# Newton of a layer norm on ScalarE with its products out of PSUM, and eleven of sixteen key tiles kept in an attention kernel

## The chip, the cores and the metric

The kernel runs on one core of a Trainium2 chip. The metric is the device time of one execution in microseconds. It was timed three times; a further execution was taken with the hardware profiler, and the profile is of that one.

## The reference, cut to what matters

The input is x, 2 batches of 2048 positions with 512 features, and one condition vector per batch. A first block (a state space layer and a feed-forward layer, both modulated by the condition) gives a new x. The change touches only the second block, an attention layer with 16 heads of 32 features:

```python
h = _sln(hidden, ...)                      # layer norm, then gamma * ln + beta from the condition
qkv = (h @ Wqkv.T + bqkv).reshape(B, N, num_heads, hd, 3)
energy = einsum('bhqd,bhkd->bhqk', q, k)
att = softmax(energy, axis=-1) / D ** 0.5  # exact: the maximum of each row is taken off first
out = einsum('bhqk,bhkd->bhqd', att, v)    # then back to (B, N, D)
h1 = out @ Wp.T + bp + hidden
h2 = _sln(h1, ...)                         # the last norm
return h2 + h1
```

All of it is in float32. The scores of one head are 2048 x 2048, so they never exist as a whole.

## The kernel before, in words

**Two parts.** The first part runs the state space layer, the feed-forward layer and the projections to queries, keys and values, chunk by chunk, and writes keys, queries and values to DRAM. It ends near 1470 us and isn't changed, but for the helper `rsqrt`, which it shares. The second part, from L698 on, is the attention and what follows it.

**Blocks.** The attention runs over 64 blocks: 2 batches, 8 pairs of heads, 4 chunks of 512 queries. In a block there are 16 tiles of 128 keys. Scores are computed with keys on the partitions: a tile of scores `s` is 128 keys x (2 heads x 512 queries), two matmuls (`raw_scores`, L754). A score plus its shift (minus the maximum of its query) goes through the exponential, and is then multiplied with the values (`weighted`, L834), which sums over keys in one PSUM bank `o`. A row of ones among the values gives the sums of the softmax.

**Two ways for a key tile.** The maximum over all keys must be known before an exponential is taken.

- The first NX = 10 tiles are *kept*: `keep` computes the scores once, ScalarE copies them to a buffer of the pool `ring` (L765), and VectorE takes a running maximum over key tiles, elementwise, from the scores in PSUM (L770, none for the first tile). Later `take_off` adds the shift in place on GpSimd (L813), and ScalarE takes the exponential (L824).
- The other NY = 6 tiles are scored *twice*: `across` computes them with queries on the partitions (two matmuls of NY x 64 = 384 columns, L779) for VectorE to reduce along the row (L784), eight times a block; `make` computes them again with keys on the partitions, and VectorE adds the shift while it leaves PSUM (L819).

`turn_run` transposes the running maximum on TensorE, one head at a time (L790), and VectorE reduces it to one column per 128 queries (L791, L794). `spread` transposes the result (pt_neg, L801), copies it out on ScalarE (neg_row, L803), and sends it through DRAM to all partitions with two DMAs on SP's queue (L805, L807); the tile that lands is the `shift`.

**Periods.** The order is written out by hand: each block has NP = 8 periods, and the loop at the end of the function goes over periods j. In period j it does, in this order: what is due at j (`after`); for the block at hand `make`; for the block AHEAD = 15 periods later one `across`; the first exponential; the `keep` of one or two tiles; the second exponential; what is due at j + 0.5 (`closing`); the take-offs for the next period; and `weighted` for the two tiles of the period before. `twice` names the two of the eight periods of keeping in which two tiles are kept; these coincide with periods that use two kept tiles and make none. So every period has two score tiles, one `across` and two tiles of weighting. Counted from the block at hand, two tiles are kept in periods 0 and 4. Each engine runs its instructions in the order in which they were written.

**PSUM.** Scores `s` have two buffers of two banks, `m` (across) one of two banks, `o` one bank, and one bank with tag `pt` serves in turn for the transposes of `turn_run` and `spread`, for projections and for the norm.

**Closing.** When all heads of a chunk are done, each tile of 128 queries is closed: `fetch` loads it, `divide` takes the softmax sums out on GpSimd, `project` multiplies with Wp (eight instructions, L905), `residual` adds x (L911), `statistics` takes mean and variance (L917, L920), `deviation` finds 1/sqrt for two query tiles at once by three Newton steps on VectorE (L932, `rsqrt` at L119 to L127, L938), `last_norm` applies scale and shift on ScalarE, and `close` multiplies by the gain row `g_row`, adds `t_row` and the residual on GpSimd and stores. Batch 0 is closed during the attention of batch 1, two query tiles in three blocks, with `add_t` on GpSimd as well. For the last batch (`LB`) the norm goes to PSUM and the gain is multiplied on VectorE (L949, L950). The last chunk is closed by `end_last`, all four tiles at once, out of PSUM.

Of the kernel before, what the change touches and what calls it, by code (L numbers as in the profile page):

```python
# [8 lines left out]
F32 = mybir.dt.float32  # L9
# [3 lines left out]
I32 = mybir.dt.int32  # L13
AF = mybir.ActivationFunctionType
ALU = mybir.AluOpType
# [24 lines left out]
def tile_s5_block_then_sln_attention(  # L40
# [48 lines left out]
    four = const.tile([P, NB], F32, name="four")  # L89

# [25 lines left out]
    def rsqrt(v, y, n, turns=(0, 3)):  # L116

        if turns[0] == 0:
            nc.vector.tensor_scalar(  # L119
                y.bitcast(I32), v.bitcast(I32), -0.5, float(0x5F3759DF), ALU.mult, ALU.add  # L120
            )
        for _ in range(*turns):
            a = small.tile([P, n], F32, name="rs_a", tag=f"rs_a{n}")
            nc.vector.tensor_mul(a, y, y)  # L124
            b = small.tile([P, n], F32, name="rs_b", tag=f"rs_b{n}")
            nc.vector.scalar_tensor_tensor(b, a, -0.5, v, ALU.mult, ALU.mult)  # L126
            nc.vector.scalar_tensor_tensor(y, b, 1.5, y, ALU.add, ALU.mult)  # L127
# [572 lines left out]
    NX = 10  # L700
# [4 lines left out]
    ring = ctx.enter_context(tc.tile_pool(name="ring", bufs=21, side="right"))  # L705
# [202 lines left out]
    def residual(b, qt):  # L908

        o4, h, py = held[b, qt]  # L910
        nc.vector.tensor_add(h, py, h)  # L911
        held[b, qt] = h, o4.rearrange("p g q -> p (g q)")

    def statistics(b, qt):
        h, ht = held[b, qt]
        st = small.tile([P, 6], F32, name="st3")
        nc.vector.bn_stats(st, h)  # L917
        if qt % 2 == 0:
            held[b, "mv"] = small.tile([P, 2, 2], F32, name="mv3")
        nc.vector.bn_aggr(held[b, "mv"][:, qt % 2, :], st)  # L920

    def add_t(b, qt):
        h, ht, *_ = held[b, qt]
        nc.gpsimd.tensor_tensor(ht, h, ending[b][1], ALU.add)

    def deviation(b, qt, parts=(0, 1)):

        mv = held[b, "mv"]
        if 0 in parts:
            v = small.tile([P, 2], F32, name="v3")  # L930
            y = small.tile([P, 2], F32, name="scale3", bufs=3)
            nc.vector.tensor_scalar(v, mv[:, :, 1], EPS, None, ALU.add)  # L932
            held[b, "vy"] = v, y
        v, y = held[b, "vy"]
        rsqrt(v, y, 2, {(0,): (0, 1), (1,): (1, 3), (0, 1): (0, 3)}[tuple(parts)])
        if 1 in parts:
            shift = small.tile([P, 2], F32, name="shift3", bufs=3)
            nc.vector.scalar_tensor_tensor(shift, mv[:, :, 0], -1.0, y, ALU.mult, ALU.mult)  # L938
            for i in range(2):
                h, ht = held[b, qt - 1 + i]  # L940
                held[b, qt - 1 + i] = h, ht, y[:, i : i + 1], shift[:, i : i + 1]

    def last_norm(b, qt):

        h, ht, scale, shift = held[b, qt]
        y = work.tile([P, D], F32, name="y")
        if b == LB:
            z = ps.tile([P, CH], F32, name="z", tag="pt")
            nc.scalar.activation(z, h, AF.Identity, bias=shift, scale=scale)  # L949
            nc.vector.tensor_tensor(y, z, ending[b][0], ALU.mult)  # L950
        else:
            nc.scalar.activation(y, h, AF.Identity, bias=shift, scale=scale)
        held[b, qt] = h, ht, y

    def close(b, qt):

        h, ht, y = held.pop((b, qt))
        if b == LB:
            ht = h
            nc.gpsimd.tensor_tensor(h, h, ending[b][1], ALU.add)  # L960
        else:
            nc.gpsimd.tensor_tensor(y, y, ending[b][0], ALU.mult)
        nc.gpsimd.tensor_tensor(y, y, ht, ALU.add)
        nc.sync.dma_start(out[b, qt * P : (qt + 1) * P, :], y)
# [65 lines left out]
    def end_last(o):  # L1030
# [17 lines left out]
        for i in range(2):  # L1048
            for t in (2 * i, 2 * i + 1):
                nc.tensor.matmul(  # L1050
                    ends["py", i][:, t % 2, :], on[:, t * P : (t + 1) * P], ends["w"], start=False, stop=True
                )
            for t in (2 * i, 2 * i + 1):
                st = small.tile([P, 6], F32, name="st3")
                nc.vector.bn_stats(st, ends["py", i][:, t % 2, :])  # L1055
                nc.vector.bn_aggr(mv[:, t, :], st)
            nc.scalar.copy(hts[i], ends["py", i])
            for t in range(2):
                nc.gpsimd.tensor_tensor(hts[i][:, t, :], hts[i][:, t, :], t_row, ALU.add)
# [6 lines left out]
        for t in range(TT):  # L1066
            qt = LC * TT + t
            y, ht = ends["h"][t // 2][:, t % 2, :], hts[t // 2][:, t % 2, :]
            nc.scalar.activation(
                y, ends["py", t // 2][:, t % 2, :], AF.Identity,  # L1070
                bias=shift[:, t : t + 1], scale=scale[:, t : t + 1],
            )
            nc.vector.tensor_tensor(y, y, g_row, ALU.mult)  # L1073
            (nc.gpsimd if t % 2 else nc.vector).tensor_tensor(y, y, ht, ALU.add)  # L1074
            nc.sync.dma_start(out[LB, qt * P : (qt + 1) * P, :], y)
# [5 lines left out]
    AHEAD = 15  # L1081
    NP = 8
    twice = (3, 7)
# [18 lines left out]
    def after(j, what, *args):  # L1102

        due.setdefault(j, []).append((what, args))
# [6 lines left out]
    FIRST = -AHEAD - 8  # L1111
    OPEN = -4
    for i, n in enumerate(opens):
        free = NP * (max(m for m in range(N) if pair_of[m] == i - 2) + 1) if i > 1 else FIRST
        after(max(free if i > 1 else FIRST, NP * n - AHEAD - 11), load_k, i)
        after(max(OPEN + 2, NP * n - 9), load_v, i)
    for n in range(N):
        after(max(FIRST + 1 + n, NP * n - AHEAD - 6), load_q, n)
        after(NP * n - AHEAD + NP + 1, turn_run, n, 0)
        after(NP * n - AHEAD + NP + 3, turn_run, n, 1)  # L1120
        after(NP * n - AHEAD + NP + 4, spread, n)
    for b in range(NB):
        for c in range(NQ):
# [22 lines left out]
            for t in range(TT):  # L1146
                qt = c * TT + t
                if b == LB:
                    k = j + 3 + 2 * t
# [148 lines left out]
```

## Time and profile before

| what | us |
|---|---|
| median of three executions (range) | 3531.95 (3527.56 to 3532.42) |
| the profiled execution | 3530.68 |
| its span, first to last instruction | 3528.9 |
| TensorE busy in the span | 3382.5 |
| VectorE, ScalarE, GpSimd busy | 2219.1, 1899.6, 2006.8 |
| first pt_neg to last pt_neg (blocks 0 to 63) | 1469.7 to 3426.0 |
| one ordinary block, pt_neg to pt_neg | 28.8 |

The page of a profile counts an engine as busy while an instruction of it runs. In a view of stretches the columns are the stretch, its length, busy time and number of instructions of TensorE matmuls, weight loads, VectorE, ScalarE and GpSimd, the granted TensorE clock as a share, the busy share of the DMA engines and GB/s. In a timeline the columns are the start, the duration, engine, source line, operation, output<-input and count; the brackets give idle time ahead of it and what ended it. In a view of waits a row says who waited for whom, for how long in total, how often, and the longest. PEld is the weight load of TensorE, which runs beside the matmul before it. The ends of matmuls are modelled, so spacing between starts tells more than their durations. L lines are those of the kernel before.

### The profile page before, as it was taken

What the parts mean: (1) busy time and instruction counts of PE and PEld (TensorE: products, weight loads), DVE (VectorE), ACT (ScalarE), POOL (GpSimd) and SP (SyncE); (2) the same over time, 40 slices, a digit from 0 to 9 for tenths busy, and PEclk for the clock granted to TensorE, in tenths of its full rate; (3) what the DMA queues carried; (4) which work ended last, traced back from release to release, by engine and by line L of the source; (5) the groups of instructions that cost most, each with busy time, mean ns of one, the idle gap of its engine ahead of it and who ended that gap; (6) DMA issues with size and microseconds to landing.
All of it is one profiled execution on the core that took longest, in us unless ns stands there. A gap on an engine that the chain in (4) does not pass through costs nothing. (4 is left out here: it accounts for less than half of the span.)

```text
span 3528.9 us, 34023 instructions
## 1 busy us (share of the span) xinstructions
PE 3382.5 (96%) x11772; PEld 1536.7 (44%) x11772; DVE 2219.1 (63%) x2946; ACT 1899.6 (54%) x2150; POOL 2006.8 (57%) x1028
## 2 busy tenths in 40 slices
PE   7999999999999999899999999999999999999986
PEld 4444444444444444444444444444444444444432
DVE  6233232323232212589999999998888888888865
ACT  2111112111111111488888888888788888888743
POOL 4223131313131311288877888888798888888765
PEclk8999999999999999999999999999999999999988
DMA  8001111111111012332313222232233323323232
GB/s 298 1 30 42 48 39 45 39 49 38 48 36 42 33 43 75 100 71 65 71 48 76 70 66 63 55 72 67 71 83 85 90 71 79 84 71 79 72 92 78
DMA packets 201539, 236.91 MB, mean 67 GB/s; under 512 B 89754, under 2 KB 118938, under 8 KB 197272
## 3 DMA queue, kind: packets, MB, share of 16 engines
q1 hardware_dynamic: 201368, 234.74, 24.4%
q8 instruction: 93, 1.52, 0.2%
q14 instruction: 78, 0.64, 0.1%
HBM read 166.77 MB, written 67.76 MB: 66 GB/s over the span
## 5 line engine op out<-in xcount | busy, mean ns | idle before, releaser
L813 POOL TENSOR_TENSOR x<-x,shift 128x1024 f32<-128x1024 f32 x640 | 1506.6, 2396 | 237.3 <-DMA shift<-flat 177.1
L765 ACT COPY x<-s 128x1024 f32<-128x1024 f32 x640 | 635.3, 1013 | 291.5 <-PE s L754 288.9
L754 PE MATMUL s<-qs,ks 128*128 128x512 f32 x2048 | 699.6, 432 | 48.1 <-DVE run L770 44.3
L824 ACT ACTIVATE x<-x 128x1024 f32<-128x1024 f32 x640 | 676.8, 1058 | 16.5 <-POOL x L813 16.5
L834 PE MATMUL o<-x,v 128*64 128x512 f32 x2560 | 673.4, 622 | 0.6 <-ACT x L824 0.6
L770 DVE TENSOR_TENSOR run<-s,run 128x1024 f32<-128x1024 f32 x512 | 625.2, 1221 | 56.6 <-ACT x L765 39.0
L819 DVE TENSOR_TENSOR pT<-s,shift 128x1024 f32<-128x1024 f32 x384 | 467.5, 1217 | 57.9 <-PE s L754 52.6
L784 DVE TENSOR_REDUCE top<-m 128x1 f32<-128x768 f32 x512 | 486.0, 949 | 25.7 <-PE m L779 25.3
L754 PEld LDWEIGHTS s<-qs,ks 128*128 128x128 f32 x2048 | 346.4, 189 | 303.9 <-DVE run L770 133.2
L488 PE MATMUL ph<-fT,w_sb 128*128 128x512 f32 x1024 | 462.4, 596 | 0.0
L501 PE MATMUL po<-w_sb,hid 128*128 128x512 f32 x1024 | 460.3, 592 | 0.0
L824 ACT ACTIVATE pT<-pT 128x1024 f32<-128x1024 f32 x384 | 407.6, 1061 | 59.2 <-DVE pT L819 51.8
L834 PE MATMUL o<-pT,v 128*64 128x512 f32 x1536 | 399.4, 598 | 13.4 <-ACT pT L824 13.4
L492 ACT ACTIVATE hid<-ph,vec 128x512 f32<-128x512 f32 x128 | 88.1, 688 | 594.8 <-PE ph L488 594.8
L159 DVE SCALAR_TENSOR_TENSOR lo<-pk,vec,hi 128x512 fp32r<-128x512 f32 x64 | 48.1, 751 | 502.7 <-ACT hi L158 497.5
L488 PEld LDWEIGHTS ph<-fT,w_sb 128*128 128x128 f32 x1024 | 192.9, 191 | 228.2 <-issue 228.2
L779 PE MATMUL m<-ks,qs 128*128 128x384 f32 x1024 | 286.1, 361 | 5.2 <-DVE top L784 3.5
L501 PEld LDWEIGHTS po<-w_sb,hid 128*128 128x128 f32 x1024 | 190.7, 190 | 221.5 <-issue 221.5
L435 POOL TENSOR_TENSOR m<-m,m 128x512 f32<-128x512 f32 x8 | 13.1, 1644 | 448.5 <-DVE m L433 448.5
L834 PEld LDWEIGHTS o<-x,v 128*64 128x64 f32 x2560 | 140.1, 137 | 265.2 <-issue 163.0
L158 ACT ACTIVATE hi<-pk,vec 128x512 fp32r<-128x512 f32 x64 | 44.0, 688 | 392.5 <-PE pk L531 392.5
L511 POOL TENSOR_TENSOR x<-x,gated 128x512 f32<-128x512 f32 x32 | 39.6, 1271 | 354.3 <-DVE gated L510 354.3
(249 smaller groups left out, 2844.9 us busy)
## 6 DMA issues: line engine op xcount, KB each, us to landing
ks<-kd SPq DMA_DIRECT2D x128, 256.0 KB
qs<-qd SPq DMA_DIRECT2D x512, 64.0 KB
shift<-flat SPq DMA_DIRECT2D x64, 512.0 KB
x<-in_x SPq DMA_DIRECT2D x8, 1024.0 KB
w_sb<-in_w SPq DMA_DIRECT2D x8, 1024.0 KB
x<-x SPq DMA_DIRECT2D x8, 1024.0 KB
kd<-hi SPq DMA_DIRECT2D x32, 256.0 KB
kd<-lo SPq DMA_DIRECT2D x32, 256.0 KB
```

The lines of the kernel that those rows point to most:

```text
L488: nc.tensor.matmul(ph, w1_sb[:, k, f * P : (f + 1) * P], fts[b, c][:, k, :], start=k == 0, stop=k == KC - 1)
L492: nc.scalar.activation(hids[f], ph, AF.Gelu_apprx_tanh, bias=vec[:, V_B1 + f : V_B1 + f + 1], scale=1.0)
L501: nc.tensor.matmul(pos[b, c][:, t, :], hid[:, t * P : (t + 1) * P], w2_sb[:, f, :], start=f == 0, stop=f == FC - 1,)
L754: nc.tensor.matmul(s[:, e, :], kst[pair_of[n], e][:, kt * P : (kt + 1) * P], qst[n][:, e, :], start=True, stop=True,)
L765: nc.scalar.copy(x, s)
L770: nc.vector.tensor_tensor(runs[n], s, kept[n, 0] if kt == 1 else runs[n], ALU.max)
L779: nc.tensor.matmul(m[:, i, :YW], qst[n][:, e, t * P : (t + 1) * P], kst[pair_of[n], e][:, k : k + YW], start=True, stop=True,)
L784: nc.vector.tensor_reduce(tops[n][:, j, 0:1], m[:, :, :YW], AX.XY, ALU.max, negate=True)
L813: nc.gpsimd.tensor_tensor(x, x, shifts[n], ALU.add)
L819: nc.vector.tensor_tensor(x, s, shifts[n], ALU.add)
L824: nc.scalar.activation(x, x, AF.Exp)
L834: nc.tensor.matmul(outs[n][64 * e : 64 * e + 64, :], v[:, kt, e : e + 2, :], x[:, e, :], start=first, stop=final,)
```

## The change

Six things change together.

- NX is 11: eleven tiles are kept, five are scored twice, `across` has two matmuls of 320 columns, and the ring has 22 buffers. AHEAD is 14, so the maxima are found 14 periods ahead. `twice` has three entries; counted from the block at hand, two tiles are kept in periods 2 (the first two tiles of a block), 5 and 7. The loads keep their old periods, now written as numbers; `spread` stays three periods ahead of its block (SPREAD), and the two halves of `turn_run` are due five and four periods ahead of it, where they were six and four.
- `statistics` serves one query tile, and with four small VectorE operations prepares the variance, a first guess, minus half the variance and minus the mean, each one column.
- `newton` replaces `deviation`: three activations on ScalarE for a step (square, 1.5 minus half the variance times it, product), and one for the shift. For batch 0 the three steps stand in three successive periods; for the last batch two and one.
- `last_norm` writes to the PSUM bank `pt` for both batches, and a new function `gain` multiplies by `g_row` and adds the residual on VectorE, the sum going to the residual's buffer. `close` adds `t_row` on GpSimd and stores; `add_t` is gone.
- In `end_last` the four additions of `t_row` ahead of the norm go; the norm stays in PSUM, VectorE multiplies and adds out of it, and `t_row` is added at the end, on GpSimd for three tiles and on VectorE for the last.
- `rsqrt` loses its argument `turns`; its uses elsewhere do the same work as before.

```diff
-    NX = 10
+    NX = 11
...
-    ring = ctx.enter_context(tc.tile_pool(name="ring", bufs=21, side="right"))
+    ring = ctx.enter_context(tc.tile_pool(name="ring", bufs=22, side="right"))
...
     def statistics(b, qt):
-        h, ht = held[b, qt]
+
+        h = held[b, qt]
         st = small.tile([P, 6], F32, name="st3")
         nc.vector.bn_stats(st, h)
...
+        mv = small.tile([P, 2], F32, name="mv3")
+        nc.vector.bn_aggr(mv, st)
+        v = small.tile([P, 1], F32, name="v3")
+        y = small.tile([P, 1], F32, name="scale3", bufs=4)
+        shift = small.tile([P, 1], F32, name="shift3", bufs=4)
+        nc.vector.tensor_scalar(v, mv[:, 1:2], EPS, None, ALU.add)
+        nc.vector.tensor_scalar(
+            y.bitcast(I32), v.bitcast(I32), -0.5, float(0x5F3759DF), ALU.mult, ALU.add
+        )
+        nc.vector.tensor_scalar(v, v, -0.5, None, ALU.mult)
+        nc.vector.tensor_scalar(shift, mv[:, 0:1], -1.0, None, ALU.mult)
+        held[b, qt] = h, y, shift, v
+
+    def newton(b, qt, turns, final):
+
+        h, y, shift, v = held[b, qt]
+        for _ in range(turns):
+            c = small.tile([P, 1], F32, name="c3")
+            nc.scalar.activation(c, y, AF.Identity, scale=y)
+            nc.scalar.activation(c, c, AF.Identity, bias=one_half, scale=v)
+            nc.scalar.activation(y, c, AF.Identity, scale=y)
+        if final:
+            nc.scalar.activation(shift, shift, AF.Identity, scale=y)
 
     def last_norm(b, qt):
 
-        h, ht, scale, shift = held[b, qt]
-        y = work.tile([P, D], F32, name="y")
-        if b == LB:
-            z = ps.tile([P, CH], F32, name="z", tag="pt")
-            nc.scalar.activation(z, h, AF.Identity, bias=shift, scale=scale)
-            nc.vector.tensor_tensor(y, z, ending[b][0], ALU.mult)
-        else:
-            nc.scalar.activation(y, h, AF.Identity, bias=shift, scale=scale)
-        held[b, qt] = h, ht, y
+        h, scale, shift, _ = held[b, qt]
+        z = ps.tile([P, CH], F32, name="z", tag="pt")
+        nc.scalar.activation(z, h, AF.Identity, bias=shift, scale=scale)
+        held[b, qt] = h, z
+
+    def gain(b, qt):
+
+        h, z = held[b, qt]
+        nc.vector.tensor_tensor(z, z, ending[b][0], ALU.mult)
+        nc.vector.tensor_tensor(h, z, h, ALU.add)
 
     def close(b, qt):
 
-        h, ht, y = held.pop((b, qt))
-        if b == LB:
-            ht = h
-            nc.gpsimd.tensor_tensor(h, h, ending[b][1], ALU.add)
-        else:
-            nc.gpsimd.tensor_tensor(y, y, ending[b][0], ALU.mult)
-        nc.gpsimd.tensor_tensor(y, y, ht, ALU.add)
-        nc.sync.dma_start(out[b, qt * P : (qt + 1) * P, :], y)
+        h, z = held.pop((b, qt))
+        nc.gpsimd.tensor_tensor(h, h, ending[b][1], ALU.add)
+        nc.sync.dma_start(out[b, qt * P : (qt + 1) * P, :], h)
...
-            for t in range(2):
-                nc.gpsimd.tensor_tensor(hts[i][:, t, :], hts[i][:, t, :], t_row, ALU.add)
...
         for t in range(TT):
+            z = ends["py", t // 2][:, t % 2, :]
+            nc.scalar.activation(
+                z, z, AF.Identity, bias=shift[:, t : t + 1], scale=scale[:, t : t + 1]
+            )
+        for t in range(TT):
             qt = LC * TT + t
...
+            y, z = hts[t // 2][:, t % 2, :], ends["py", t // 2][:, t % 2, :]
+            nc.vector.tensor_tensor(z, z, g_row, ALU.mult)
+            nc.vector.tensor_tensor(y, z, y, ALU.add)
+            (nc.gpsimd if t < TT - 1 else nc.vector).tensor_tensor(y, y, t_row, ALU.add)
             nc.sync.dma_start(out[LB, qt * P : (qt + 1) * P, :], y)
...
-    AHEAD = 15
+    AHEAD = 14
     NP = 8
-    twice = (3, 7)
+    twice = (0, 3, 5)
...
-        after(NP * n - AHEAD + NP + 3, turn_run, n, 1)
-        after(NP * n - AHEAD + NP + 4, spread, n)
+        after(NP * n - AHEAD + NP + 2, turn_run, n, 1)
+        after(NP * n + SPREAD, spread, n)
...
                 if b == LB:
-                    k = j + 3 + 2 * t
+                    k = j + (3 if c == LC - 1 else 4) + 2 * t
...
-                    if t % 2:
-                        after(k + 4, deviation, b, qt)
-                        after(k + 5, last_norm, b, qt - 1)
-                        closing(k + 5, last_norm, b, qt)
-                        after(k + 6, close, b, qt - 1)
-                        closing(k + 6, close, b, qt)
+                    closing(k + 3, newton, b, qt, 2, False)
+                    closing(k + 4, newton, b, qt, 1, True)
+                    closing(k + 4, last_norm, b, qt)
+
+                    if c < LC - 1 and (k + 5 - SPREAD) % NP == NP - 1:
+                        due.setdefault(k + 5, []).insert(0, (gain, (b, qt)))
+                    else:
+                        closing(k + 5, gain, b, qt)
+                    closing(k + 6, close, b, qt)
...
-                    after(k + 9, add_t, b, qt)
-                    if t % 2:
-                        closing(k + 8, deviation, b, qt, (0,))
-                        closing(k + 9, deviation, b, qt, (1,))
-                        closing(k + 10, last_norm, b, qt - 1)
-                        closing(k + 11, last_norm, b, qt)
-                        after(k + 12, close, b, qt - 1)
-                        after(k + 14, close, b, qt)
+                    for i in range(3):
+                        closing(k + 8 + i, newton, b, qt, 1, i == 2)
+
+                    k += 2 if t % 2 else 8
+                    closing(k + 10, last_norm, b, qt)
+                    closing(k + 11, gain, b, qt)
+                    after(k + 13, close, b, qt)
```

More of the change, by code (lines that the diff above doesn't have):

```diff
@@ L89, in tile_s5_block_then_sln_attention @@
     four = const.tile([P, NB], F32, name="four")
+    one_half = const.tile([P, 1], F32, name="one_half")
+    nc.gpsimd.memset(one_half, 1.5)
     mod = const.tile([P, N_MOD, KC, NB], F32, name="mod")
@@ L113, in per_feature, with rsqrt @@
         return vec[:, at : at + KC].unsqueeze(2).to_broadcast([P, KC, NB])
[L116 to L122, printed above, removed]
+    def rsqrt(v, y, n):
+        nc.vector.tensor_scalar(
+            y.bitcast(I32), v.bitcast(I32), -0.5, float(0x5F3759DF), ALU.mult, ALU.add
+        )
+        for _ in range(3):
             a = small.tile([P, n], F32, name="rs_a", tag=f"rs_a{n}")
@@ L911, in residual @@
         nc.vector.tensor_add(h, py, h)
-        held[b, qt] = h, o4.rearrange("p g q -> p (g q)")
+        held[b, qt] = h
     def statistics(b, qt):
-        h, ht = held[b, qt]
+        h = held[b, qt]
         st = small.tile([P, 6], F32, name="st3")
         nc.vector.bn_stats(st, h)
[L918 to L941, printed above, removed]
@@ new lines, in statistics @@
+        nc.vector.bn_aggr(mv, st)
[3 more added lines that the diff above has]
+        nc.vector.tensor_scalar(v, mv[:, 1:2], EPS, None, ALU.add)
+        nc.vector.tensor_scalar(
+            y.bitcast(I32), v.bitcast(I32), -0.5, float(0x5F3759DF), ALU.mult, ALU.add
+        )
+        nc.vector.tensor_scalar(v, v, -0.5, None, ALU.mult)
+        nc.vector.tensor_scalar(shift, mv[:, 0:1], -1.0, None, ALU.mult)
@@ L1066, in end_last @@
         for t in range(TT):
-            qt = LC * TT + t
[L1068 to L1074, printed above, removed]
+            z = ends["py", t // 2][:, t % 2, :]
+            nc.scalar.activation(
+                z, z, AF.Identity, bias=shift[:, t : t + 1], scale=scale[:, t : t + 1]
+            )
+        for t in range(TT):
+            qt = LC * TT + t
+            y, z = hts[t // 2][:, t % 2, :], ends["py", t // 2][:, t % 2, :]
+            nc.vector.tensor_tensor(z, z, g_row, ALU.mult)
+            nc.vector.tensor_tensor(y, z, y, ALU.add)
+            (nc.gpsimd if t < TT - 1 else nc.vector).tensor_tensor(y, y, t_row, ALU.add)
             nc.sync.dma_start(out[LB, qt * P : (qt + 1) * P, :], y)
-    AHEAD = 15
+    AHEAD = 14
     NP = 8
-    twice = (3, 7)
+    twice = (0, 3, 5)
     keeps, m = [], 0
@@ L1111, in tile_s5_block_then_sln_attention @@
     FIRST = -AHEAD - 8
+    SPREAD = -3
     OPEN = -4
@@ L1114, in tile_s5_block_then_sln_attention @@
         free = NP * (max(m for m in range(N) if pair_of[m] == i - 2) + 1) if i > 1 else FIRST
-        after(max(free if i > 1 else FIRST, NP * n - AHEAD - 11), load_k, i)
+        after(max(free if i > 1 else FIRST, NP * n - 26), load_k, i)
         after(max(OPEN + 2, NP * n - 9), load_v, i)
     for n in range(N):
-        after(max(FIRST + 1 + n, NP * n - AHEAD - 6), load_q, n)
+        after(max(FIRST + 1 + n, NP * n - 21), load_q, n)
         after(NP * n - AHEAD + NP + 1, turn_run, n, 0)
-        after(NP * n - AHEAD + NP + 3, turn_run, n, 1)
-        after(NP * n - AHEAD + NP + 4, spread, n)
+        after(NP * n - AHEAD + NP + 2, turn_run, n, 1)
+        after(NP * n + SPREAD, spread, n)
     for b in range(NB):
```

## The prediction

> **What bounds the kernel now.** I read the busy table, then stretches by stage, then one ordinary block instruction by instruction, then the waits of the last stage. The busy table:
>
> ```profile
> PE 3382.5 (96%) x11772; PEld 1536.7 (44%) x11772; DVE 2219.1 (63%) x2946; ACT 1899.6 (54%) x2150; POOL 2006.8 (57%) x1028
> ```
>
> The means mix stages. Busy time by stretch (TensorE, weight loads, VectorE, ScalarE, GpSimd):
>
> ```profile
> 1499.20:2453.60 954.40, 934.63 (x3996) 424.11 (x3994) 865.42 (x863) 848.47 (x925) 780.88 (x332) 1.00 0.28 66
> 2453.60:3261.50 807.90, 776.61 (x3171) 348.57 (x3169) 699.87 (x795) 659.07 (x719) 665.85 (x314) 0.99 0.33 78
> 3261.50:3528.90 267.40, 218.22 (x747) 89.68 (x745) 186.13 (x262) 137.22 (x154) 181.08 (x103) 0.90 0.28 80
> 2021.70:2050.50 28.80, 28.29 (x123) 12.84 (x121) 26.20 (x27) 25.69 (x29) 23.05 (x11) 1.00 0.29 60
> ```
>
> Stage I is 33 attention blocks of 28.8 us, stage II 25 blocks with the closing of batch 0 among them (32.3 us each), stage III the closing of batch 1 and the end. In I and II TensorE sets the pace, with VectorE and ScalarE at about 90%. Its only idle time in a block follows a period with two kept tiles (timeline around 2048; start, duration):
>
> ```profile
> 2047.18 0.60 PE L779 MATMUL m<-ks,qs 128*128 128x384 f32 x2
> 2047.62 1.10 PE L754 MATMUL s<-qs,ks 128*128 128x512 f32 x4
> 2048.28 1.93 ACT L765 COPY x<-s 128x1024 f32<-128x1024 f32 x2 [0.30 <-PE s L754]
> 2049.33 2.55 DVE L770 TENSOR_TENSOR run<-s,run 128x1024 f32<-128x1024 f32 x2
> 2050.52 0.27 PE L801 MATMUL pt_neg<-ident,neg 128*8 128x128 f32 x1
> 2051.06 0.24 ACT L803 COPY neg_row<-pt_neg 8x128 f32<-8x128 f32 x1
> 2051.94 0.74 PE L754 MATMUL s<-qs,ks 128*128 128x512 f32 x2 [0.26 <-DVE run L770]
> ```
>
> The second maximum ends at 2051.88 and frees the score bank that TensorE wants from about 2051.53: 0.41 us lost, and 0.1 for restarting. This happens twice a block, and one of them loses 0.1 more: 1.1 us of 28.8.
>
> In stage II and III the Newton steps of the last norm (L932 to L938) stand on VectorE before work that TensorE waits for. Stage II, once per pair of query tiles; then stage III, where each small operation waits for a whole GpSimd one:
>
> ```profile
> 2746.80 0.73 PE L754 MATMUL s<-qs,ks 128*128 128x512 f32 x2 [1.62 <-DVE run L770]
> ...
> 3457.11 2.29 DVE L119 TENSOR_SCALAR scale<-v 128x2 int32<-128x2 int32 x1
> 3460.65 2.28 DVE L126 SCALAR_TENSOR_TENSOR rs_b<-rs_a,v 128x2 f32<-128x2 f32 x1
> 3465.27 0.16 DVE L124 TENSOR_TENSOR rs_a<-scale 128x2 f32<-128x2 f32 x1
> ...
> 3468.94 1.97 PE L834 MATMUL o<-pT,v 128*64 128x512 f32 x4 [5.57 <-ACT pT L824]
> ```
>
> TensorE's own waits from 3300 on that come from this:
>
> ```profile
> PE o L834 <- ACT pT L824: 13.4, 6, 5.6
> PE pt_run L790 <- DVE y L950: 8.2, 2, 6.1
> PE py L905 <- DVE top L784: 5.4, 2, 3.4
> ```
>
> **What the Trainium skill says.** "SBUF — State Buffer", Who interferes with whom: a VectorE operation with two SBUF inputs, or in a two-port mode, waits for a whole GpSimd operation. The trace agrees: 0.16 us alone, up to 2.29 behind a take-off. "VectorE: DVE Perf Modes", Mode 2×_2P: that mode wants the outermost non-unit dimension even, or odd and equal. For one column this decides nothing; the trace's 16 single-column copies (L453) took 143 to 155 ns, many beneath GpSimd additions (at 161.47 beneath one from 160.85 to 162.57), so I take one-column, one-input operations as free of the wait. "ScalarE: Activation LUTs", What ACT_TABLE_LOAD costs: 186 ns fixed, 93 more for each per-partition operand, 0.833 ns an element, which gives 0.80 us for the last norm's 512 elements; measured 0.77 to 0.81.
>
> **The change part by part.** *Eleven kept.* Per block: one score pair moves from make to keep (TensorE 0), one maximum more and one shift-subtraction less on VectorE (1.22 each, 0), one copy more on ScalarE (1.01, or 0.92 overlapped: 25.7 to 26.6 of 28.8), one take-off more on GpSimd (2.37: 23.05 to 25.4). The first take-off starts 6.1 us after pt_neg (2021.70 to 2027.78) and eleven take 26.0; the next block's shift comes 28.8 later, so GpSimd still idles 2.8 and exponentials stay fed. The sixteen maxima matmuls shrink from 384 to 320 columns: two take 0.35 us, four 512-column ones about 1.0, so 0.457 ns a column, 0.146 each, 0.029 saved, **0.45 us a block**. A floor from weight loads would show at 0.11 (four 128-column transposes in 0.41), which isn't reached. Their reduce drops from 0.949 to 0.82 (512 elements take 0.690): VectorE gains 1.0, which is cover, not path.
>
> *New places.* Two-copy periods are now 2, 5 and 7 of a block. In 2 the first tile has no maximum, so nothing queues. In 5 the spread's copy (neg_row) now stands before the first exponential: it can start 0.31 after pt_neg (3369.94 to 3370.25) and takes 0.24, so the first copy starts 1.41 after the period's start, not 1.19. Both maxima end 0.22 later: TensorE loses 0.32 + 0.45 + 0.1 after period 5, and 0.12 + 0.45 + 0.1 after period 7, 1.54 in place of 1.12. Reaching these waits sooner costs 0.08 of the saving: **+0.50**. Net +0.05 a block. Ends: -0.45 if neg_row fits in, +0.5 if every two-copy period slips by another quarter us. Moving the maxima by a period passes no DMA on SP's queue: the loads of keys and queries stay in their periods, and so does the spread with its two transfers; the store of a finished tile stays one transfer, from the residual's buffer. Stage I: 33 x 0.05 = **+1.6 us**.
>
> *Stage II, per three blocks (two query tiles).* Columns -1.35, stalls +1.5. The projection (8 instructions, 4.3 us a tile) stands at the start of periods 6, 7, 0 and 1. Today it covers one stall (0.5 a tile); now it covers both (1.5): -2.0. The deviation on VectorE goes: 8 times 1.62 on the scores and 5.5 on pt_neg in the stage, -2.3 per three blocks. The statistics gain, per tile, four one-column operations of 0.2 with gaps, at the end of period 2, ahead of two periods in which VectorE is full: +1.6. Newton on ScalarE: ten activations a tile, 0.25 with one operand and 0.34 with two, 3.3 us with their own waits (estimate from that page and the 0.77 row). Two turns fall into periods 3 and 4, where ScalarE idles 0.4 to 0.8. The third with the scaled shift falls behind period 5, beneath a projection for one tile; for the other it stands with the 0.77 norm before the exponentials of period 6: +1.8, and the gain's two VectorE operations (2 x 0.69) +0.5. GpSimd loses two of four 1.29 us operations a tile, hidden either way. Sum -0.25, times 8.3: **-2 us** (both ends: -15, +15).
>
> *Stage III.* Of the 13.4 + 5.4 us of waits behind deviations I let a third stay, because statistics and gain still stand before work on VectorE: -12.5. The turning's 8.2 stays nearly: for one tile in four the gain now precedes a turning in period 4 and waits for Newton and norm on ScalarE, about 3.7 twice. **-12**. At the end four GpSimd additions no longer run beneath rsqrt (0.44, 1.19, 1.18, 1.19 us where 0.16 is due: -3.3). Thirteen operations of 0.2 then end at 3515.6, the first norm 0.8 later; behind it VectorE has eight operations of 0.65 and one last addition of 0.7, to about 3522.4, where today's last addition ends at 3525.9: **-3.4** in all, the 3.3 included.
>
> Sum 1.6 - 2 - 12 - 3.4 = -15.8. The profiled execution took 3530.7 around a span of 3528.9, the median is 3531.95; so 3516.
>
> **Rivals.** *ScalarE's order becomes the bound (slower).* Five of eight periods (5, 6, 7, 0, 2) hold an extra copy, neg_row or raw; if the delay of period 5 isn't made up before 7, each block loses about 0.45 more: 58 x 0.45 = +26, **3542**. It decides from 0.27 us a block on. For it: three two-copy periods in six. Against: one-copy periods leave ScalarE 0.43 idle. *One-column operations do wait for GpSimd (slower).* Today's pairs pay 1.1 + 0.5 us (means 1284 and 623 ns over 0.16); 28 tiles at 1.6, two thirds of it on the path: +30, **3546**. *The stalls vanish (faster):* the shorter reduce frees the banks and 58 blocks keep 0.45 more: **3490**. *It cancels:* stage III keeps its waits because gain and Newton replace deviation: **3530**.
>
> **How the numbers follow.** Forecast 0.42 (own range 3503 to 3529), ScalarE 0.20, one-column waits 0.12, vanishing stalls 0.13, cancelling 0.13. I call within 0.2% (7 us) the same, about what a measurement of this kernel can tell. Faster: nine tenths of the forecast and the vanishing stalls, with a little of the rest, 0.52. Same 0.16, slower 0.32. For eight in ten the range takes 3490 at the low end and 3552 at the high.
>
> **What would show it.** Ordinary blocks of 28.85 us; maxima matmuls 0.15 apart; TensorE waiting about 0.3 then 0.45 after period 5; neg_row 0.31 after pt_neg; the four one-column operations at 0.16 us; stage III near 252 us; no wait of o for pT over 2 us. Wrong if blocks reach 29.3 (ScalarE's order), or one-column operations show 2.3 us.

## The result: 4.1% slower, all of it in the attention blocks

The kernel took 3674.93 us after the change (3667.42 to 3675.92) against 3529.76 before (medians of four executions each), a ratio of 1.0407 with a 95% interval of 1.0395 to 1.0420. The forecast was 3516 with a range to 3552, so both the time and its sign were missed. The profiled execution took 3667.42 us around a span of 3665.6.

The busy table of the changed kernel:

```profile
PE 3411.3 (93%) x11772; PEld 1496.6 (41%) x11772; DVE 2133.2 (58%) x2937; ACT 2036.3 (56%) x2494; POOL 2090.9 (57%) x1046
```

TensorE fell from 96% to 93% and VectorE from 63% to 58%, and ScalarE rose to 56% only: no engine became full, they wait more. In the views of the changed kernel, L lines are its own: L755 for scores, L766 for the copy, L771 for the running maximum, L835 for the weighting. Busy time by stretch, with the same limits as before (33 blocks, 25 blocks, the rest, and one ordinary block):

```profile
1499.80:2559.20 1059.40, 962.40 (x3995) 404.76 (x3993) 827.42 (x863) 879.83 (x958) 859.71 (x367) 1.00 0.25 60
2559.20:3399.30 840.10, 782.31 (x3172) 331.59 (x3170) 677.91 (x796) 722.72 (x904) 681.94 (x307) 1.00 0.31 75
3399.30:3665.60 266.30, 212.21 (x745) 85.48 (x743) 161.35 (x252) 177.96 (x279) 172.21 (x93) 0.95 0.28 80
2013.60:2045.70 32.10, 29.15 (x123) 12.28 (x121) 25.01 (x27) 26.64 (x30) 25.23 (x11) 1.00 0.44 103
```

Stage I is 105.0 us longer, stage II 32.2 us, stage III 1.1 us shorter. An ordinary block is 32.10 us and not 28.80, and in it ScalarE has 26.64 us of work, just the 26.6 forecast. So the work was priced rightly and a wait was missed. The view of waits names it:

```profile
DVE run L771 <- ACT x L766: 409.8, 441, 2.5
PEld s L755 <- DVE run L771: 373.3, 541, 1.9
ACT x L766 <- PE o L835: 293.1, 346, 4.4
PE s L755 <- DVE run L771: 153.4, 363, 1.0
ACT x L766 <- PE s L755: 39.5, 58, 8.3
```

Read from the third line: the copy of a kept tile (L766) waits for `o`, the weighting matmuls, 346 times. From the copy it goes on to the running maximum, and from there to the score banks and TensorE. Before, the same copy waited for its own scores only, when ScalarE had nothing else to do:

```profile
ACT x L765 <- PE s L754: 288.9, 420, 5.6
```

A copy has no use for `o`. But it writes to a ring buffer, and that buffer must have been read by the weighting of the tile that lay in it. The timeline of the changed kernel shows it in a two-copy period and in the next period with one copy:

```profile
2014.15 1.46 PE L755 MATMUL s<-qs,ks 128*128 128x512 f32 x4
...
2015.06 0.98 ACT L766 COPY x<-s 128x1024 f32<-128x1024 f32 x1
...
2015.54 1.08 PE L835 MATMUL o<-x,v 128*64 128x512 f32 x4
...
2016.45 1.03 PE L835 MATMUL o<-pT,v 128*64 128x512 f32 x4
...
2016.72 1.01 ACT L766 COPY x<-s 128x1024 f32<-128x1024 f32 x1 [0.68 <-PE o L835]
...
2017.77 1.23 DVE L771 TENSOR_TENSOR run<-s,run 128x1024 f32<-128x1024 f32 x1 [0.47 <-ACT x L766]
...
2019.05 0.73 PE L755 MATMUL s<-qs,ks 128*128 128x512 f32 x2 [0.61 <-DVE run L771]
...
2020.89 1.01 ACT L766 COPY x<-s 128x1024 f32<-128x1024 f32 x1 [1.25 <-PE o L835]
```

Both score tiles of the first period start in the group at 2014.15. The second copy could follow the first at 2016.04; it starts at 2016.72, when the four matmuls of the first weighted tile are through (the next four start at 2016.45).

**Why the ring does this.** Buffers are taken in turn. With 22 of them and eleven tiles a block, tile kt of block n gets the buffer of tile kt of block n-2. Call that older tile the predecessor. With n the number of the block, tile kt is kept in period 8n-14+i and its predecessor is weighted in period 8n-15+k; the table gives i and k:

| kt | 0 | 1 | 2 | 3 | 4 | 5 | 6 | 7 | 8 | 9 | 10 |
|---|---|---|---|---|---|---|---|---|---|---|---|
| i | 0 | 0 | 1 | 2 | 3 | 3 | 4 | 5 | 5 | 6 | 7 |
| k | 0 | 1 | 2 | 2 | 3 | 4 | 5 | 5 | 6 | 7 | 7 |

Where k = i+1, the predecessor is weighted in the very period in which the new tile is copied: kt 1, 2, 5, 6, 8 and 9, six of eleven. In TensorE's order the weighting stands behind the new scores, so the copy must wait past its own scores for about half a period's weighting. That is what the trace has in stage I: 198 such waits in 33 blocks, six each. In stage II it has 126 of a possible 150, and 22 elsewhere. Before, with ten tiles and 21 buffers, tile kt got the buffer of tile kt-1 two blocks back, which was weighted at least one period earlier.

### The profile page after: what moved, and what is told of

It reads as the page before. It is cut to its first block, busy times and chain, and to the rows that moved or that the text cites. A ratio compares the mean times of both kernels' runs of the same rounds, so it can differ in the third digit from the quotient of the medians.

```text
span 3665.6 us, 34404 instructions
## 1 busy us (share of the span) xinstructions
PE 3411.3 (93%) x11772; PEld 1496.6 (41%) x11772; DVE 2133.2 (58%) x2937; ACT 2036.3 (56%) x2494; POOL 2090.9 (57%) x1046
## 5 line engine op out<-in xcount | busy, mean ns | idle before, releaser
L814 POOL TENSOR_TENSOR x<-x,shift 128x1024 f32<-128x1024 f32 x704 | 1650.1, 2387 | 318.5 <-DMA shift<-flat 289.4
L766 ACT COPY x<-s 128x1024 f32<-128x1024 f32 x704 | 707.4, 1008 | 332.9 <-PE o L835 293.1
L771 DVE TENSOR_TENSOR run<-s,run 128x1024 f32<-128x1024 f32 x576 | 704.4, 1223 | 290.7 <-ACT x L766 280.0
L755 PE MATMUL s<-qs,ks 128*128 128x512 f32 x2048 | 719.0, 438 | 160.9 <-DVE run L771 153.4
L825 ACT ACTIVATE x<-x 128x1024 f32<-128x1024 f32 x704 | 726.5, 1055 | 6.0 <-POOL x L814 6.0
L835 PE MATMUL o<-x,v 128*64 128x512 f32 x2816 | 718.0, 611 | 5.3 <-ACT raw L844 5.3
L755 PEld LDWEIGHTS s<-qs,ks 128*128 128x128 f32 x2048 | 318.4, 189 | 442.1 <-DVE run L771 373.3
L785 DVE TENSOR_REDUCE top<-m 128x1 f32<-128x640 f32 x512 | 417.4, 815 | 6.9 <-PE m L780 6.8
L820 DVE TENSOR_TENSOR pT<-s,shift 128x1024 f32<-128x1024 f32 x320 | 388.8, 1215 | 11.1 <-PE s L755 9.2
L825 ACT ACTIVATE pT<-pT 128x1024 f32<-128x1024 f32 x320 | 340.5, 1064 | 29.1 <-DVE pT L820 25.7
L835 PE MATMUL o<-pT,v 128*64 128x512 f32 x1280 | 329.5, 593 | 1.7 <-ACT pT L825 1.7
L835 PEld LDWEIGHTS o<-x,v 128*64 128x64 f32 x2816 | 156.5, 135 | 304.0 <-issue 163.6
L780 PE MATMUL m<-ks,qs 128*128 128x320 f32 x1024 | 263.8, 339 | 9.7 <-DVE top L785 7.3
```

The lines of the kernel that those rows point to most:

```text
L755: nc.tensor.matmul(s[:, e, :], kst[pair_of[n], e][:, kt * P : (kt + 1) * P], qst[n][:, e, :], start=True, stop=True,)
L766: nc.scalar.copy(x, s)
L771: nc.vector.tensor_tensor(runs[n], s, kept[n, 0] if kt == 1 else runs[n], ALU.max)
L780: nc.tensor.matmul(m[:, i, :YW], qst[n][:, e, t * P : (t + 1) * P], kst[pair_of[n], e][:, k : k + YW], start=True, stop=True,)
L785: nc.vector.tensor_reduce(tops[n][:, j, 0:1], m[:, :, :YW], AX.XY, ALU.max, negate=True)
L814: nc.gpsimd.tensor_tensor(x, x, shifts[n], ALU.add)
```

## Experiments

All ratios are to the kernel before, run beside on the same chip (medians 3527.14 to 3527.51 us). Block lengths are from one pt_neg to the next in an ordinary block.

**1. One buffer more.**

```diff
-    qpool = ctx.enter_context(tc.tile_pool(name="qpool", bufs=4, side="right"))
-    ring = ctx.enter_context(tc.tile_pool(name="ring", bufs=22, side="right"))
+    qpool = ctx.enter_context(tc.tile_pool(name="qpool", bufs=3, side="right"))
+    ring = ctx.enter_context(tc.tile_pool(name="ring", bufs=23, side="right"))
...
-        after(max(FIRST + 1 + n, NP * n - 21), load_q, n)
+        after(max(FIRST + 1 + n, NP * n - 17), load_q, n)
```

> The changed kernel with one ring buffer more (23 for 22); to make room, three query buffers for four, their loads four periods later (17 ahead of the block for 21). Ring theory: with 22 buffers and eleven tiles a block a buffer goes from key tile kt of block n-2 to key tile kt of block n, and for six of the eleven tiles the old occupant is weighted in the very period in which the new one is copied, behind the copy's scores in TensorE's order. With 23 the old occupant was weighted a period before at the latest. So no ScalarE copy waits for o (346 such waits, 293 us, in the changed kernel), the ordinary block falls from 32.10 us to 28.9 (28.7 to 29.3), the total to 3515-3540. Rival (ScalarE's order: three two-copy periods, neg_row ahead of the copies): the block stays at 31 us or more and the total above 3630, with the wait merely renamed from o to s.

3523.63 us, ratio 0.9988 (0.9980 to 0.9997). No copy waits for `o` any more; it waits for its own scores, as before the change. That wait, the stretches and the block:

```profile
ACT x L766 <- PE s L755: 180.7, 259, 8.3
```

```profile
1502.60:2457.10 954.50, 926.80 (x3996) 407.28 (x3995) 830.25 (x863) 872.76 (x958) 856.04 (x364) 1.00 0.26 66
2457.10:3264.90 807.80, 766.37 (x3171) 332.94 (x3169) 676.07 (x795) 719.93 (x904) 683.20 (x307) 1.00 0.31 78
3264.90:3522.90 258.00, 213.53 (x745) 87.24 (x743) 161.50 (x251) 177.38 (x279) 174.04 (x94) 0.94 0.28 85
2022.96:2051.78 28.82, 28.01 (x123) 12.34 (x121) 25.10 (x27) 26.43 (x30) 25.80 (x12) 1.00 0.26 60
```

The block is 28.82 us with the same work on each engine. 104.9 us of stage I, 32.3 of stage II and 8.3 of stage III come back, 2.8 go to a later start of the first blocks: the ring costs 142.7 us of span (3665.6 to 3522.9), a little more than the 136.7 that the change lost. The rival, ScalarE's order with three two-copy periods, falls, since all of that order is still there.

**2. Was it the loads of queries?** The first experiment also moved these. Here only they move, and the ring has 22.

```diff
-    qpool = ctx.enter_context(tc.tile_pool(name="qpool", bufs=4, side="right"))
+    qpool = ctx.enter_context(tc.tile_pool(name="qpool", bufs=3, side="right"))
...
-        after(max(FIRST + 1 + n, NP * n - 21), load_q, n)
+        after(max(FIRST + 1 + n, NP * n - 17), load_q, n)
```

> The changed kernel with 22 ring buffers and only the side edit of the first experiment, three query buffers with loads 17 periods ahead of the block. Ring theory: the ordinary block stays at 32.1 us and the total at 3665-3680, so the fall to 28.82 us in the first experiment is the twenty-third buffer's. If the loads of queries had a part in it, the total is below 3640.

One execution: 3675.73 us, block 32.10, and the same 346 waits (294.4 us). The loads have no part in it.

**3. The same fault put into the kernel before.**

```diff
-    ring = ctx.enter_context(tc.tile_pool(name="ring", bufs=21, side="right"))
+    ring = ctx.enter_context(tc.tile_pool(name="ring", bufs=20, side="right"))
```

> The kernel before with one ring buffer less (20 for 21), nothing else. Ring theory: with 20 buffers and ten tiles a block the buffer goes from (n-2, kt) to (n, kt); for kt 0, 4, 5 and 9 the old occupant is weighted in the period of the new copy. Four copies a block wait for o, where none does now; at the 0.54 us a waiting copy costs in the changed kernel (3.25 us a block over six) the ordinary block rises from 28.8 to about 31.0 and the total to about 3655 (3600-3690). Rival (the loss is of the three two-copy periods or of the longer ScalarE work): within 0.3% of before, 3520-3540.

3590.37 us, ratio 1.0182 (1.0167 to 1.0197), block 30.04. One buffer less makes the kernel before slower by 63 us, with four waits a block where there were none:

```profile
ACT x L765 <- PE o L834: 213.0, 246, 4.9
ACT x L765 <- PE s L754: 135.6, 238, 5.6
```

The mechanism was right, the size half of what was expected: 1.24 us a block for four waits. The two lines suggest why. The copies' waits for `o` (213.0) took the place of waits for their scores, which fell from 288.9 to 135.6: 153.3 of the 213 was idle time of ScalarE anyway. The rest, 59.7, is about the 60.4 us by which the span grew. In the changed kernel 293.1 replaces 141.2 (180.7 with 23 buffers, 39.5 with 22) and 151.9 stays, against 142.7 of span. In both kernels, then, the price of these waits was not their length but about what they exceed the idle time already there. With three two-copy periods ScalarE has less of that: 0.41 us of span for a wait, against 0.25 in the kernel before.

**4. The order, with no buffer more.** Maxima 13 periods ahead make every copy one period later, so no predecessor is weighted in its period.

```diff
-    AHEAD = 14
+    AHEAD = 13
...
-        after(NP * n - AHEAD + NP + 1, turn_run, n, 0)
-        after(NP * n - AHEAD + NP + 2, turn_run, n, 1)
+        closing(NP * n - AHEAD + NP, turn_run, n, 0)
+        closing(NP * n - AHEAD + NP + 1, turn_run, n, 1)
```

> The changed kernel with the maxima 13 periods ahead in place of 14, ring of 22 as it was, everything else but the half-period places of the two turnings of the running maximum as in the change; two tiles are kept in periods 3, 6 and 0 of the block at hand. Ring theory: every copy now comes a period later than in the change, and every old occupant of its buffer has been weighted at least one period before, so no copy waits for o: block 28.7-29.5 us, total 3515-3550. Since no memory is added here, this separates the order from the number of buffers. Rival (ScalarE's order): still three two-copy periods, one with neg_row ahead of it, so 31 us or more and above 3630.

3581.14 us, ratio 1.0158 (1.0141 to 1.0175), block 30.02. The waits for `o` are gone with 22 buffers, but a new one stands in the block, of the experiment's own making, because the second turning is now half a period ahead of the spread:

```profile
2020.46 0.27 PE L802 MATMUL pt_neg<-ident,neg 128*8 128x128 f32 x1 [1.32 <-DVE neg L795]
```

30.02 less 28.82 is 1.20, about this wait. Another run left the turnings where the change has them, five and four periods ahead of the block:

```diff
-    AHEAD = 14
+    AHEAD = 13
...
-        after(NP * n - AHEAD + NP + 1, turn_run, n, 0)
-        after(NP * n - AHEAD + NP + 2, turn_run, n, 1)
+        after(NP * n - 5, turn_run, n, 0)
+        after(NP * n - 4, turn_run, n, 1)
```

> The changed kernel with the maxima 13 periods ahead in place of 14 and nothing else: 22 buffers, the turnings of the running maximum at the starts of the periods five and four ahead of the block, as in the change. The earlier run with 13 had them half a period later, and pt_neg then waited 1.32 us a block for neg. Ring theory: no copy waits for o and pt_neg does not wait; the block is 28.7-29.0 us (28.82 with 23 buffers) and the total 3512-3530. If the first turning, now one period after the last kept tile, waits for the running maximum, that shows as pt_run waiting for run, up to 1 us: 29.0-29.8 and 3530-3570.

3579.99 us, ratio 1.0145 (1.0128 to 1.0162), block 29.58: the alternative of the expectation, though above its total. No copy waits for `o`; the turning waits for the running maximum. TensorE's waits from 1500 to 2450:

```profile
PE s L755 <- DVE run L771: 26.3, 87, 3.1
PE pt_run L791 <- DVE run L771: 17.2, 31, 0.6
```

That is 0.55 us a block of the 0.76 over 28.82; the rest stays open. So 13 periods cure the ring, but leave the chain from last maximum to shift one period short. At 14 periods the copy waits for a buffer, at 13 the turning waits for a result.

**5. The closing part alone** (Newton on ScalarE, products out of PSUM, the new end), with the schedule and the ring of before:

```diff
-    NX = 11
+    NX = 10
...
-    AHEAD = 14
+    AHEAD = 15
-    twice = (0, 3, 5)
+    twice = (3, 7)
```

The ring has 21 buffers, and the turnings stay five and four periods ahead of the block.

> The closing part of the change alone: Newton on ScalarE, products out of PSUM, the new end; with ten kept tiles, 15 periods ahead, two two-copy periods and 21 ring buffers as before (the turnings of the running maximum at five and four periods ahead of the block, as in the change). By the terms of the prediction without the schedule's: stage II +1.6 per three blocks (+13), stage III -12, the end -3.4, so -2: 3528; if stage III keeps its waits (-1, as the changed kernel shows) 3537; if the closing's stalls in stage II hide, 3515. Ring theory: the ordinary block is 28.8 as before, and the whole loss of 145 us is absent. Rival (closing part at fault for a part of the loss): above 3550.

3536.39 us, ratio 1.0028 (1.0017 to 1.0040); the three stages:

```profile
1498.91:2454.81 955.90, 935.25 (x3996) 425.65 (x3994) 863.23 (x863) 848.40 (x925) 779.28 (x332) 1.00 0.26 66
2454.81:3272.41 817.60, 777.16 (x3171) 345.60 (x3170) 704.97 (x795) 700.38 (x879) 625.17 (x282) 1.00 0.31 77
3272.41:3534.66 262.25, 212.60 (x747) 89.53 (x745) 166.23 (x253) 173.66 (x274) 159.80 (x88) 0.94 0.27 82
```

By itself this part is a small loss: stage II +9.7, stage III with the end -5.2. The 145 us are not its doing. The prediction's terms without the schedule had +13 and -15.4: the first of the right size, the second three times too good. Against this run, the schedule with 23 buffers (experiment 1) takes 9.8 off stage II and 4.2 off stage III. The first has the sign of the prediction's schedule terms for that stage (-1.35, +1.5 and -2.0 per three blocks, about -15). That projections covering the stalls bring it, as the prediction argued, was not tested.

**6. The weighting ahead of the copies.** TensorE's order in a period is made scores, across, weighting, scores; a first tile of two is kept where other periods have their make.

```diff
+        if len(todo) == 2:
+            keep(n, todo.pop(0))
         if n is not None:
             across(n, i // TT, i % TT)
         if now is not None:
             exponentials(now, uses[k][0])
+        past, before = block_at(j - 1)
+        if past is not None:
+            for h, kt in enumerate(uses[before]):
+                weighted(past, kt, before == 0 and h == 0, before == NP - 1 and h == 1)
         for kt in todo:
             keep(n, kt)
```

The weighting at the end of the loop goes.

> The changed kernel with its 22 ring buffers; in a period the order on TensorE is first score tile, across, the four pairs of weighting matmuls of the period before, then the (second) kept tile; in a two-copy period the first of the two tiles is kept ahead of across. Ring theory: the six tiles that wait for a weighting of their own period (the second tile of each pair and three single ones) now find it ahead of their scores, so no copy waits for o, and the 32.10 us block goes to 29 or less without a buffer more, the total below 3530. If the waits go by the count of buffers alone and not by TensorE's order, it stays above 3600. Risk to both: the weighting comes half a period earlier and may wait for its exponentials, which would show as o waiting for x or pT, 0.3-1 us a period.

> Both: 23 ring buffers and the order of scores, across, weighting, scores. Against the run that has 23 buffers and only the early first tile it tells whether the weighting half a period earlier costs or gains. If score tiles evenly apart are what TensorE needs, 27.4-27.9 us a block and 3440-3475; if the exponentials are then late, 28.5 or more and above 3500.

3718.97 us with 22 buffers (ratio 1.0543, 1.0527 to 1.0559) and 3717.02 with 23 (1.0537, 1.0519 to 1.0554); blocks 32.02 and 31.98. In neither run does a copy wait for `o`, so with 22 buffers too that wait goes when the weighting stands ahead of the scores in TensorE's order. The total doesn't show it: it lies above 3600, where the expectation had put the count of buffers alone. With 23 buffers it is the same within 0.1%, so another wait sets the pace here. It is the risk that was named: the weighting waits for its exponentials. Waits of the run with 22 buffers from 1500 to 2500:

```profile
PEld o L835 <- ACT pT L825: 135.4, 157, 1.2
ACT x L766 <- PE s L755: 135.4, 124, 1.6
```

Now TensorE and ScalarE wait for each other in turn, about 4.0 us a period.

**7. Can the remaining stalls be had?** With 23 buffers TensorE still loses time after the maxima, as the prediction priced it. The timeline of experiment 1, from the spread on:

```profile
2022.96 0.27 PE L802 MATMUL pt_neg<-ident,neg 128*8 128x128 f32 x1
...
2023.27 0.26 ACT L804 COPY neg_row<-pt_neg 8x128 f32<-8x128 f32 x1
...
2024.39 1.89 ACT L766 COPY x<-s 128x1024 f32<-128x1024 f32 x2
...
2025.41 2.55 DVE L771 TENSOR_TENSOR run<-s,run 128x1024 f32<-128x1024 f32 x2 [0.67 <-ACT x L766]
...
2027.26 0.45 PE L780 MATMUL m<-ks,qs 128*128 128x320 f32 x2
...
2028.02 0.73 PE L755 MATMUL s<-qs,ks 128*128 128x512 f32 x2 [0.31 <-DVE run L771]
```

The first maximum starts at 2025.41, 0.03 us after the first copy ends in the trace (2025.38), though it needs nothing from it. The program makes two readers of one PSUM bank take turns; the Trainium skill, "PSUM — Partial Sum Buffer", section PSUM bank collisions raise a hardware error, says that the engines may not access one bank in the same partition at the same time and that the compiler's scheduler makes instructions of different engines on one bank depend on each other, two reads too. The trace agrees: the maximum was released by the copy. So a copy queued behind an exponential holds the maximum back. Two orders were tried against this. First, the first tile of a pair ahead of across (the first two added lines of experiment 6 alone), on 23 buffers and on the kernel before:

> The changed kernel with 23 ring buffers (as the first experiment), and in a two-copy period the first of the two tiles is kept ahead of across, where a period with make has its make; so scores, maxima, scores come in turn. With the ring out of the way the block is 28.82 us, in which TensorE loses 0.46 twice between the next period's maxima and its scores, and about 0.25 between the two tiles of a two-copy period: the waits that the prediction priced. If they come from two running maxima queued one behind the other, the new order ends them and the block falls to 27.6-28.0 us, the total to 3450-3480. If VectorE or ScalarE paces the block in truth (both over 90% busy in it), the block stays within 0.3 of 28.8 and the total at 3510-3530.

> The kernel before with only that order: in a two-copy period the first tile is kept ahead of across. It asks whether the two losses of 0.41-0.5 us a block that the prediction started from (1.1 us a block in all) are due to the order inside a period. If so the block falls from 28.8 to 27.7-28.0 and the total to 3465-3490; if not, 3520-3535. It also tells how much of a gain of the version with eleven tiles is the order alone.

Both miss: 3564.73 us (ratio 1.0106, 1.0091 to 1.0121) and 3561.07 (1.0094, 1.0079 to 1.0109), blocks 29.58 and 29.42. The timeline of the first shows one place where it goes wrong:

```profile
2014.16 1.02 ACT L766 COPY x<-s 128x1024 f32<-128x1024 f32 x1 [0.57 <-PE s L755]
...
2015.21 1.22 DVE L771 TENSOR_TENSOR run<-s,run 128x1024 f32<-128x1024 f32 x1 [1.32 <-ACT x L766]
...
2016.36 0.82 DVE L785 TENSOR_REDUCE top<-m 128x1 f32<-128x640 f32 x1
```

The early tile's maximum now stands ahead of the reduce on VectorE, and VectorE idles 1.32 us for the copy with the reduce behind it. Then, both copies ahead of the first exponential on ScalarE, TensorE's order as it was:

```diff
+        if len(todo) == 2:
+            keep(n, todo.pop(0))
+            keep(n, todo.pop(0))
         if now is not None:
             exponentials(now, uses[k][0])
```

> The changed kernel with 23 ring buffers (as the first experiment), and in a two-copy period both tiles are kept ahead of the first exponential on ScalarE (TensorE's order stays). The maximum of a tile starts 0.03 us after the end of its copy in every pair of the profile, so it queues behind ScalarE: with 23 buffers the first copy of a two-copy period waits for an exponential and starts about 0.5 us after its scores, and VectorE idles 0.67 us. If this delay is what makes TensorE lose 0.46 twice a block, both maxima end some 0.5 us sooner now, the block falls from 28.82 to 27.9-28.4 and the total to 3470-3505. If ScalarE, 26.4 us busy in the block, cannot take the idle time that the early copies bring (0.3-0.4 us three times), the block stays at 28.6-29.3 and the total is 3510-3550.

> The kernel before with the same order: in its two two-copy periods both copies ahead of the first exponential. If the two losses of TensorE in a block (0.5 and 0.6 us) come from copies queued behind an exponential, the block falls from 28.80 to 27.9-28.4 and the total to 3475-3505. If the maxima are held by VectorE alone, it stays at 28.7-29.0 and 3520-3540.

On 23 buffers 3517.60 us, ratio 0.9973 (0.9962 to 0.9984); on the kernel before 3541.42, ratio 1.0044 (1.0029 to 1.0059); blocks 28.70 and 28.96. The first has the lowest median of this study, 0.3% below the kernel before, but its block gained 0.1 and not the 0.4 to 0.9 expected. A block has two pairs of copies with two maxima, in periods 5 and 7. Here they are with the new order:

```profile
2021.38 1.93 ACT L766 COPY x<-s 128x1024 f32<-128x1024 f32 x2 [0.65 <-PE s L755]
...
2022.43 2.56 DVE L771 TENSOR_TENSOR run<-s,run 128x1024 f32<-128x1024 f32 x2 [0.35 <-ACT x L766]
...
2028.69 1.93 ACT L766 COPY x<-s 128x1024 f32<-128x1024 f32 x2 [0.67 <-PE s L755]
...
2029.73 2.55 DVE L771 TENSOR_TENSOR run<-s,run 128x1024 f32<-128x1024 f32 x2 [0.69 <-ACT x L766]
```

And this is the pair of period 7 in experiment 1, whose scores start at 2030.95:

```profile
2031.66 1.93 ACT L766 COPY x<-s 128x1024 f32<-128x1024 f32 x2
...
2032.71 2.55 DVE L771 TENSOR_TENSOR run<-s,run 128x1024 f32<-128x1024 f32 x2 [0.73 <-ACT x L766]
```

In period 5 VectorE idles 0.35 us where it idled 0.67, and TensorE loses 0.24 after it where it lost 0.46 (from the start of the maxima matmuls to that of the scores it is 0.54, 0.76 in experiment 1, and 0.30 of that is the matmuls). In period 7 nothing changes. With 23 buffers the first copy already started 0.71 us after its scores, and it starts 0.73 after them now (2027.96 to 2028.69), so no exponential held it; VectorE idles about as long as before, and TensorE still loses 0.46. So copies behind an exponential explain a part of one of the two losses, and not both. Why the same order loses in the kernel before was not followed up.

## Why the prediction was wrong, step by step

- **The failed step** is the one on eleven kept tiles: "one copy more on ScalarE (1.01, or 0.92 overlapped: 25.7 to 26.6 of 28.8)" at no cost. It priced how long the copy runs and let it wait for scores alone. The ring's growth from 21 to 22 buffers was described and never costed: the moved maxima were followed past SP's queue and past ScalarE's order, but not to the tile that has to leave the buffer first. Shown: 346 waits for `o`, 142.7 us of span, which a buffer more removes and a buffer less brings into the kernel before.
- **Stage I, +1.6.** With 23 buffers it is 954.5 us where it was 954.4, with blocks of 28.82 (forecast 28.85). Its parts hold as well: the matmuls of the maxima are 0.14 to 0.15 apart (0.146); neg_row starts 0.31 after pt_neg in the timeline of experiment 7; between the maxima matmuls and the scores TensorE loses 0.46 after period 5 and again after period 7 (0.45). As a forecast for the change it failed by 103 us.
- **ScalarE's order, the rival at 3542**, had the right sign and the watch line was crossed ("blocks reach 29.3"), but for another reason: the same order with one buffer more runs at 28.82.
- **Stage II, -2.** With 23 buffers 807.8 against 807.9; the closing part alone +9.7 (estimate +13), the schedule -9.8. That the sum comes out near zero is in part luck: both terms were smaller than forecast (9.7 for 13, 9.8 for about 15), and the two errors cancel.
- **One-column operations** took 0.143 to 0.156 us, also beneath GpSimd additions. That rival (3546) falls; the single-column copies of the first part were a fair guide. Newton on ScalarE runs at 0.28 to 0.29 us with one operand and 0.39 with two, where 0.25 and 0.34 were estimated.
- **Stage III, -12.** The waits of `o` for the exponentials did go: 13.4 us before, 1.7 after. But the turning of the running maximum waits longer, now for the gain, four times and not twice. From 3399.3 on, in the changed kernel:

```profile
PE pt_run L791 <- DVE xr L955: 14.3, 4, 4.8
PE o L835 <- ACT pT L825: 1.7, 2, 1.1
```

  The prediction let the old 8.2 us "nearly" stay, as 3.7 twice (with the 12.5 this adds to 13.3, where it wrote 12). With 23 buffers stage III is 258.0, so -9.4 together with the end, where -15.4 was forecast.
- **The end, -3.4.** From the first statistics to the last addition it takes 13.87 us (3648.58 to 3662.45), 16.36 before (3509.54 to 3525.90): -2.5. All small operations ran at 0.16 to 0.17, as forecast. What was missed is that the first product waits for two norms, not one: it starts at 3656.05, when the second norm of the same two-bank tile ends. The eight operations from it on also start 0.71 us apart, where 0.65 was reckoned.

```profile
3654.22 0.16 DVE L1060 SCALAR_TENSOR_TENSOR shift<-mv,scale 128x4 f32<-128x4 f32 x1
3656.05 0.70 DVE L1069 TENSOR_TENSOR py<-py,g_row 128x512 f32<-128x512 f32 x1 [1.66 <-ACT py L1063]
```

The forecast without the ring would have been about 10 us too good: -15.8 against -6.0 of span (3522.9 from 3528.9). 2.9 of that is a later first pt_neg (1472.6 for 1469.7), which the prediction did not speak of.

## What to carry to other kernels

When a change puts more tiles through a pool, write down for each tile which older tile leaves its buffer, in which step its last reader runs, and whether that reader stands before or behind the new writer's source on the reader's engine; a pool with an exact multiple of the tiles can tie each tile to the step in which it is least ready. The same table tells the one buffer, or the one step of distance, that unties them. In these two kernels, a wait added on an engine with idle time cost about what it exceeded that idle time, so the same fault cost more in the fuller schedule (0.41 us a wait against 0.25).

## What the runs showed that was not expected

- One buffer of 4 KB a partition is worth 142.7 us of span in the changed kernel (3665.6 to 3522.9) and 60.4 in the kernel before (3528.9 to 3589.3 without it).
- The maximum over a score tile follows the copy of the same tile, though both only read it: with 23 buffers none of the 640 maxima starts before that copy has ended, and the closest start 0.03 us behind it. So a copy and a maximum of 1.0 and 1.2 us hold a score tile for at least 2.2 us, not for 1.2.
- At the end, a product on VectorE out of one bank of a two-bank PSUM tile started only 0.03 us after ScalarE's norm in the other bank had ended: 1.66 us of idle time, some 0.8 of it for the second norm. The runs don't show why the tile counts as one.
